# Softmax sums of two groups in one run: batched denominators in the attention of an eight-image bottleneck kernel

## The chip, the cores and the metric

The kernel runs on one core of a Trainium2 chip. The metric is device time in microseconds (us) of one execution; the figure shown for a kernel is the median of its runs. Engines are named as the profile names them: PE is TensorE (matmul), PEld its weight loads, DVE VectorE, ACT ScalarE, POOL GpSimd, and SP SyncE, whose queue issues most transfers. A matrix product in float32 goes through PE in two passes; the profile shows each pass as a record, so 8 records are 4 products.

## The reference

Eight images of 512 x 32 x 32 are normalised in groups of 16 channels, go through a convolution block with two attention bottlenecks, and are added to the input:

```python
def cbs(x, w, p, pad):
    return jax.nn.silu(bn_eval(conv2d(x, w, pad), p))

t = cbs(x, cv1_w, cv1_bn, 0)                  # 512 -> 512, split in two halves of 256 channels
ys = [t[:, :C], t[:, C:]]
for i in range(N):                            # N = 2 bottlenecks
    yi = ys[-1]
    z = cbs(yi, m_cv1_w[i], m_cv1_bn[i], 1)   # 3x3
    z = bot_attention(z, m_qkv_w[i], m_rw[i], m_rh[i])
    z = jax.nn.silu(bn_eval(conv2d(z, m_cv2_w[i], 0), m_cv2_bn[i]))
    ys.append(yi + z)
return cbs(jnp.concatenate(ys, axis=1), cv2_w, cv2_bn, 0)

# bot_attention: 4 heads of 64 channels over 1024 positions
logits = jnp.einsum('bhdi,bhdj->bhij', q, k + r) * HD ** (-0.5)
a = jax.nn.softmax(logits, axis=-1)
out = jnp.einsum('bhij,bhdj->bhdi', a, v)
# the whole: x + conv_block(group_norm(x)), group_norm over 16 channels x 1024 positions
```

The softmax's denominators are sums over the 1024 keys, one for each head and query position. The kernel takes exponentials without a maximum, multiplies by v first, and divides the result afterwards.

## The kernel before

**Rounds and attentions.** The images go in four rounds, p = 0 to 3, each with a pair: image A (`ia`) and image B (`ib`). In a round there are four attentions, in this order: A with n = 0 (first bottleneck), B with n = 0, A with n = 1, B with n = 1; 16 in all. Around each one lie the 3x3 convolution (as a Winograd product), the projection to q, k and v (as a Strassen product) and, after it, the second 1x1 product `m2` (L1270). While an attention runs, steps of other work are laid between its parts: in A and B with n = 0 the group norm of the next round's images, and in B, n = 0, the pieces that turn image A's result into Winograd tiles. The first attention of round 0 takes a path of its own to its end (`at_once`).

**One attention** (`attention_fast`, L1014) has four groups, 0 to 3: channel block c = 0 or 1 (two heads each) and half of the query positions. A group has eight key blocks, worked in four pairs. For each pair: `logits` (L1037) puts q k products in a PSUM tile of the pool with tag "big" (three tiles), ACT takes the exponentials into two `pt` tiles (L1041), `add_up` (L1055, L1057) adds them on DVE into `acc` (two buffers), and, one pair later in PE's order, `times_v` (L1071) multiplies by v into the one `av` tile of another PSUM pool. PE's order is thus logits of pair i + 1, then v of pair i.

**Border of two groups.** After a group's last v product its result is evicted: ACT copies one half of `av` (L1078), DVE adds the other (L1079); the next group's first v product needs the tile. The first `add_up` of the next group is placed behind that eviction. Ahead of the next group's first v product, PE runs `sums(g)` (L1083 to L1096): four products of a block of ones with `acc`, each on 32 columns of the array, sum it over the partitions into `s_ps`, also in the pool "big".

**From the sums to the division.** ACT copies `s_ps` to `s_row` (L1094), SP writes four rows of it to a DRAM tile (L1095). Two pairs later `spread` reads them back as 128 x 8 (`total`, L1124), DVE inverts them (L1131), SP writes them to `r_dram` (L1133) and reads each back twice (L1135), broadcast over the 64 channels of a head. `scale` (L1143) multiplies the evicted result; it is placed in the second pair of the group but one after. The last group's `sums`, `spread` and `scale` are called by the code behind the attention (`end.sums()` and so on), which puts them among the work that follows, ahead of `m2`.

**Order of work.** Instructions of an engine run in the order in which they stand in its queue. `tc.issue_after(x)` puts what follows behind instruction x in the scheduler's order. `behind` is a table of hooks: the key g, or (g, pair), names the v product behind which a step of other work is placed. `NORM_A` and `NORM_B` are the keys at which one step of the group norm (`step_norm`) is placed: four of statistics (two of `bn_stats` and one of `bn_aggr` on DVE), then the mean (`gn_mean`: a small product into a tile of the pool "big", `gm`, four DVE instructions), then `gn_rstd` (a product, `gr` L744 on DVE, a power on POOL L745, the shift on POOL L802, L803), and then the applies on ACT (L809), of which A has four of 1024 elements and B eight of 512. `at_keys` are the keys of the tile pieces (`step_part`) in B, n = 0.

Of the kernel before, what the change touches and what calls it, by code (L numbers as in the profile page):

```python
# [44 lines left out]
F32 = mybir.dt.float32  # L45
# [16 lines left out]
def kernel(  # L62
# [428 lines left out]
    def stages(act, small, ps_big, ps_av, n_pt):  # L491
# [522 lines left out]
        def attention_fast(qkv, ao, at, behind, at_once=False):  # L1014
# [66 lines left out]
            def sums(g):  # L1081

                NQ4 = HALF // 2  # L1083
                ps = ps_big.tile([P, NQ4], F32, tag="big", name="s_ps")
                acc = accs.pop(g)
                for at_q in range(4):
                    hd, part = divmod(at_q, 2)
                    nc.tensor.matmul(  # L1088
                        ps[at_q * 32 : (at_q + 1) * 32, :], ones[:, 0:32], acc[:, hd, ts(part, NQ4)],
                        start=True, stop=True, tile_position=(0, at_q * 32),  # L1090
                    )
                s_dram = tc.dram_tile([4, NQ4], F32, name=f"s_dram{at + g}")
                row = act.tile([P, NQ4], F32, tag="h", name="s_row", bufs=2)
                nc.scalar.copy(row, ps)  # L1094
                nc.sync.dma_start(s_dram, row[0:P:32, :])  # L1095
                return s_dram  # L1096
# [25 lines left out]
            def total(g, s_dram):  # L1122

                nc.sync.dma_start(sums_all[:, at + g, :], s_dram.rearrange("a (i r) -> (a i) r", r=QP))  # L1124
                return sums_all[:, at + g, :]

            def spread(g, s_dram):

                rs = act.tile([P, HALF], F32, tag="rs", name="rs", bufs=4)
                rc = small.tile([P, QP], F32, tag="rc", name="rc", bufs=2)  # L1130
                inverted[0] = nc.vector.reciprocal(rc, total(g, s_dram))  # L1131
                r_dram = tc.dram_tile([2, HALF], F32, name=f"r_dram{at + g}")
                nc.sync.dma_start(r_dram.rearrange("h (i r) -> (h i) r", r=QP), rc)  # L1133
                for hd in range(2):
                    spread_out[0] = nc.sync.dma_start(  # L1135
                        rs[hd * HD : (hd + 1) * HD, :], r_dram[hd : hd + 1, :].to_broadcast([HD, HALF])
                    )
                return rs
# [5 lines left out]

            NQ = NJ // PAIR
# [674 lines left out]
    for p in range(NP):  # L1820
# [255 lines left out]
        def step_part():  # L2076
            next(parts_at, None)
# [286 lines left out]
```

## Time and profile before

| | us |
|---|---|
| median of three runs (lowest, highest) | 2253.76 (2253.61, 2255.59) |
| the profiled execution | 2252.28 |
| its span in the trace | 2250.8 |
| PE busy | 2209.8 |
| PE: logits L1037, v products L1071 | 486.4, 485.9 |
| PE: sums L1088 (504 records) | 40.3 |
| DVE busy | 1728.8 |
| ACT busy | 1101.3 |
| POOL busy | 225.1 |

The profile is one execution. "L1088 PE MATMUL s_ps<-acc,ones ... x504 | 40.3, 391 | 2.2 <-DVE gm" reads: 504 records of line 1088 on PE that write `s_ps` from `acc` and `ones`, 40.3 us busy, 391 ns each in the mean (records overlap, since matmuls are pipelined), 2.2 us of idle time of the engine ahead of them, most of which ended with `gm` on DVE. A timeline row has start, duration, engine, line and operation; x8 in it means eight records in a row. In brackets behind a row stands the idle time ahead of it and what ended it. PE's clock was granted at 0.998 of full speed over the span.

### The profile page before, as it was taken

Reading aid. Unit: us, or ns where it says so; the run is one execution under the profiler, and the core shown is the slowest. Engines: PE = TensorE matmul, PEld = TensorE weight load, DVE = VectorE, ACT = ScalarE, POOL = GpSimd, SP = SyncE. Lnnn points to the kernel's source line nnn. Section 1 sums busy time; section 2 is a strip of 40 time slices with the busy share of each in tenths; the row PEclk is TensorE's granted clock in tenths of the full one; section 3 lists DMA queues with packets and bytes.
Section 4 is the critical chain, followed back from the end, with each engine's and each line's share of the span. In section 5 each row is a group of like instructions: output and inputs, shape, how many; then the busy total and the mean of one; then the engine's idle time right before and its main releaser. Section 6 shows DMA issues by size and latency. Waiting matters only on the chain.

```text
span 2250.8 us, 40563 instructions
## 1 busy us (share of the span) xinstructions
PE 2209.8 (98%) x16346; PEld 1079.1 (48%) x16346; DVE 1728.8 (77%) x2675; ACT 1101.3 (49%) x1359; POOL 225.1 (10%) x417
## 2 busy tenths in 40 slices
PE   7999999999999999999999999999999999999998
PEld 3653437343474445633447343654345733473443
DVE  7988879878678688877947868986794868796652
ACT  7554653644225765465324667355622455335533
POOL 4322210000220000000021000000012000000001
PEclk9999999999999999999999999999999999999999
DMA  9855447221581324521257151632136611351214
GB/s 276 309 157 150 155 148 260 91 93 50 135 269 59 113 88 143 178 64 65 66 154 260 30 173 35 198 111 82 51 79 176 226 44 34 102 192 35 67 46 111
DMA packets 135284, 285.63 MB, mean 127 GB/s; under 512 B 34512, under 2 KB 62156, under 8 KB 134064
## 3 DMA queue, kind: packets, MB, share of 16 engines
q1 hardware_dynamic: 103184, 197.34, 26.5%
q0 software_dynamic: 31904, 85.61, 13.2%
q8 instruction: 131, 2.15, 0.4%
q14 instruction: 65, 0.53, 0.1%
HBM read 214.86 MB, written 68.03 MB: 126 GB/s over the span
## 4 chain that ended last, share of the span: by engine, by line
PE 82%; DVE 11%; issue 3%; ACT 2%; DMA 1%; POOL 0%; SPq 0%; DVEq 0%; POOLq 0%; ACTq 0%
PE av_ps L1071 17%; PE l_ps L1037 16%; PE c L1290 9%; PE c_ps L653 7%; PE c_new L1290 6%; PE p_ps L916 6%; PE ps L523 5%; PE m_ps L1270 5%; PE x_ps L1390 4%; PE p_ps L922 3%; DVE acc L1057 1%; PE s_ps L1088 1%; PE p_ps L886 1%; DVE c_e L680 1%; ACT ypad L495 0%
## 5 line engine op out<-in xcount | busy, mean ns | idle before, releaser
L1041 ACT ACTIVATE pt<-l_ps 128x1024 f32<-128x1024 f32 x512 | 495.7, 1023 | 339.5 <-PE l_ps L1037 228.0
L1057 DVE TENSOR_TENSOR acc<-acc,pt 128x1024 f32<-128x1024 f32 x384 | 469.7, 1223 | 60.4 <-ACT pt L1041 34.9
L1037 PE MATMUL l_ps<-q,kr 64*64 64x512 f32 x4096 | 486.4, 590 | 2.4 <-ACT pt L1041 1.5
L1071 PE MATMUL av_ps<-pt,vT 64*64 64x512 f32 x4096 | 485.9, 591 | 1.8 <-DVE z L1079 1.5
L1037 PEld LDWEIGHTS l_ps<-q,kr 64*64 64x64 f32 x4096 | 158.0, 133 | 272.1 <-issue 251.0
L1071 PEld LDWEIGHTS av_ps<-pt,vT 64*64 64x64 f32 x4096 | 155.1, 133 | 275.3 <-issue 250.6
L653 PE MATMUL c_ps<-v_in,u 128*64 128x128 f32 x4320 | 239.1, 273 | 2.5 <-issue 2.5
L653 PEld LDWEIGHTS c_ps<-v_in,u 128*64 128x64 f32 x4320 | 235.8, 137 | 9.3 <-issue 9.3
L1270 PE MATMUL m_ps<-z,m_sb 128*128 128x512 f32 x256 | 112.5, 592 | 0.0
L658 ACT COPY c_m<-c_ps 128x512 f32<-128x512 f32 x48 | 28.1, 586 | 169.9 <-PE c_ps L653 153.1
L916 PE MATMUL p_ps<-t_z,sq 128*128 128x512 f32 x224 | 107.0, 595 | 0.0
L1079 DVE TENSOR_TENSOR z<-av_ps,z 128x512 f32<-128x512 f32 x64 | 44.0, 688 | 73.5 <-ACT z L1078 73.4
L495 ACT ACTIVATE t<-m_ps,bh,sh 128x512 f32<-128x512 f32 x64 | 46.3, 774 | 86.5 <-PE m_ps L1270 86.5
L916 PE MATMUL p_ps<-z,sq 128*128 128x512 f32 x168 | 80.1, 604 | 4.4 <-ACT z L495 4.3
L1055 DVE TENSOR_TENSOR acc<-pt 128x1024 f32<-128x1024 f32 x64 | 77.8, 1216 | 6.8 <-ACT pt L1041 6.8
L1340 POOL DMA_DIRECT2D c_out<-in_x_dram x56 | 50.3, 972 | 280.2 <-ACT c_out L495 276.8
L1270 PEld LDWEIGHTS m_ps<-z,m_sb 128*128 128x128 f32 x256 | 48.3, 190 | 58.8 <-issue 57.4
L1143 DVE TENSOR_TENSOR z<-z,rs 128x512 f32<-128x512 f32 x64 | 43.9, 686 | 26.0 <-DMA rs<-r_dram 25.9
L495 ACT ACTIVATE c_out<-cz,bh,sh 128x512 f32<-128x512 f32 x14 | 16.7, 1294 | 90.4 <-DVE cz L1367 90.4
L495 ACT ACTIVATE z<-z,bh,sh 128x512 f32<-128x512 f32 x64 | 47.7, 804 | 25.0 <-DVE z L704 24.3
L1390 PE MATMUL x_ps<-t_x,sw 128*128 128x512 f32 x128 | 55.9, 592 | 0.0
L922 PEld LDWEIGHTS p_ps<-sq,z 128*128 128x128 f32 x336 | 42.9, 191 | 26.3 <-issue 12.5
(313 smaller groups left out, 3153.7 us busy)
## 6 DMA issues: line engine op xcount, KB each, us to landing
u<-u SPq DMA_DIRECT2D x135, 512.0 KB
rs<-r_dram SPq DMA_DIRECT2D x126, 128.0 KB
sq<-sq SPq DMA_DIRECT2D x42, 384.0 KB
x<-in_x_dram SPq DMA_DIRECT2D x28, 512.0 KB
r_in<-r SPq DMA_DIRECT2D x28, 512.0 KB
y_in<-y SPq DMA_DIRECT2D x28, 512.0 KB
c_out<-in_x_dram POOLq DMA_DIRECT2D x56, 256.0 KB, 5.4
out_dram<-c_out POOLq DMA_DIRECT2D x56, 256.0 KB, 3.7
```

The costliest lines, as they stand in the source:

```text
L495: silued[0] = nc.scalar.activation(dst, src, AF.Silu, scale=sh[:, k : k + 1], bias=bh[:, k : k + 1])
L523: last_product[0] = nc.tensor.matmul(ps[:, half, :], w_of(k), rhs_of(k, half), start=(k == begin), stop=(k == end))
L653: conv_product[0] = nc.tensor.matmul(to[o], us[cp][:, k, row, c, o], rhs, start=(k == 0), stop=(k == NM - 1),)
L916: nc.tensor.matmul(ps[:, o, :], w[:, o, :], rhs, start=not onto, stop=True, skip_group_check=onto)
L922: nc.tensor.matmul(v[:, ts(j, P)], rhs[:, ts(j, P)], w[:, 2, :], start=j == 0 and not onto, stop=True, skip_group_check=True,)
L1037: nc.tensor.matmul(ps[kh * HD : (kh + 1) * HD, hd, :], kr[r, c, o : o + HD], q[r, c, ts(half, HALF)], start=True, stop=True,)
L1041: last_exp[0] = exp = nc.scalar.activation(pt, ps, AF.Exp, scale=SCALE)
L1057: ins = nc.vector.tensor_tensor(accs[g], accs[g], pt[i], ALU.add)
L1071: nc.tensor.matmul(avs[g][hd * HD : (hd + 1) * HD, kh, :], vT[r, j, o : o + HD], pt[i][r, hd, :], start=(j == 0), stop=(j == NJ - 1),)
L1270: nc.tensor.matmul(pss[half][:, oc, :], m2_sb[:, n, k, ts(oc, P)], ao[:, k, ts(half, HALF)], start=(k == 0), stop=(k == NM - 1),)
L1290: nc.tensor.matmul(ps[:, o, :], w[:, k, ts(o, P)], rhs[part][:, c], start=(k == 0 and not onto), stop=(k == KB - 1), skip_group_check=onto,)
L1390: nc.tensor.matmul(ps[:, o, :], w[:, c, ts(o, P)], rhs[c], start=(c == 0 and not onto), stop=(c == 1), skip_group_check=onto,)
```

## The change

`sums`, `total`, `spread` and `scale_all` now take a list of groups. A table `batch` says after which group which list is summed: groups 0 and 1 together, and groups 2 and 3 together; with `at_once`, and with the new argument `apart`, which B's attention with n = 0 sets, groups 2 and 3 are summed one by one, as before. A list of two groups has one `s_ps` tile of 128 x 2 x 256 and eight products in it, one copy, one transfer each of `s_dram`, `sums_all` and `r_dram`, one reciprocal of 128 x 16, and, as before, two broadcast transfers and one scale for each group. A group's sums that are batched stand where those of the list's last group stood.

A hook ("border", g) is called between the eviction of group g - 1 and the first `add_up` of group g; B's attention with n = 0 places tile pieces there, and two keys of `at_keys` are dropped. In `NORM_A` and `NORM_B` the first step moves from (0, 2) to (0, 1); in `NORM_A` (1, 3) is dropped and (3, 1) is new.

```diff
@@ -1011,7 +1011,7 @@
 
             return q, kr, vT, later
 
-        def attention_fast(qkv, ao, at, behind, at_once=False):
+        def attention_fast(qkv, ao, at, behind, at_once=False, apart=False):
 
             q, kr, vT, later = qkv
             behind.get(-1, lambda: None)()
@@ -1078,21 +1078,22 @@
                     nc.scalar.copy(dst, av[:, 0])
                     evicted[0] = nc.vector.tensor_tensor(dst, av[:, 1], dst, ALU.add)
 
-            def sums(g):
+            def sums(gs):
 
                 NQ4 = HALF // 2
-                ps = ps_big.tile([P, NQ4], F32, tag="big", name="s_ps")
-                acc = accs.pop(g)
-                for at_q in range(4):
-                    hd, part = divmod(at_q, 2)
-                    nc.tensor.matmul(
-                        ps[at_q * 32 : (at_q + 1) * 32, :], ones[:, 0:32], acc[:, hd, ts(part, NQ4)],
-                        start=True, stop=True, tile_position=(0, at_q * 32),
-                    )
-                s_dram = tc.dram_tile([4, NQ4], F32, name=f"s_dram{at + g}")
-                row = act.tile([P, NQ4], F32, tag="h", name="s_row", bufs=2)
+                ps = ps_big.tile([P, len(gs), NQ4], F32, tag="big", name="s_ps")
+                for n, g in enumerate(gs):
+                    acc = accs.pop(g)
+                    for at_q in range(4):
+                        hd, part = divmod(at_q, 2)
+                        nc.tensor.matmul(
+                            ps[at_q * 32 : (at_q + 1) * 32, n, :], ones[:, 0:32], acc[:, hd, ts(part, NQ4)],
+                            start=True, stop=True, tile_position=(0, at_q * 32),
+                        )
+                s_dram = tc.dram_tile([len(gs), 4, NQ4], F32, name=f"s_dram{at + gs[0]}")
+                row = act.tile([P, len(gs), NQ4], F32, tag="h", name="s_row", bufs=2)
                 nc.scalar.copy(row, ps)
-                nc.sync.dma_start(s_dram, row[0:P:32, :])
+                nc.sync.dma_start(s_dram.rearrange("g a i -> a g i"), row[0:P:32])
                 return s_dram
 
             def last_sums(g):
@@ -1119,29 +1120,38 @@
                 nc.sync.dma_start(cs, s_dram.rearrange("k h (i r) -> (h i) k r", r=QP))
                 nc.vector.tensor_tensor(sums_all[:, at + g, :], cs[:, 0], cs[:, 1], ALU.add)
 
-            def total(g, s_dram):
-
-                nc.sync.dma_start(sums_all[:, at + g, :], s_dram.rearrange("a (i r) -> (a i) r", r=QP))
-                return sums_all[:, at + g, :]
-
-            def spread(g, s_dram):
-
-                rs = act.tile([P, HALF], F32, tag="rs", name="rs", bufs=4)
-                rc = small.tile([P, QP], F32, tag="rc", name="rc", bufs=2)
-                inverted[0] = nc.vector.reciprocal(rc, total(g, s_dram))
-                r_dram = tc.dram_tile([2, HALF], F32, name=f"r_dram{at + g}")
-                nc.sync.dma_start(r_dram.rearrange("h (i r) -> (h i) r", r=QP), rc)
-                for hd in range(2):
-                    spread_out[0] = nc.sync.dma_start(
-                        rs[hd * HD : (hd + 1) * HD, :], r_dram[hd : hd + 1, :].to_broadcast([HD, HALF])
-                    )
-                return rs
+            def total(gs, s_dram):
+                dst = sums_all[:, at + gs[0] : at + gs[0] + len(gs), :]
+                nc.sync.dma_start(dst, s_dram.rearrange("g a (i r) -> (a i) g r", r=QP))
+                return dst
+
+            def spread(gs, s_dram):
+
+                rc = small.tile([P, len(gs), QP], F32, tag="rc", name="rc", bufs=2)
+                inverted[0] = nc.vector.reciprocal(rc, total(gs, s_dram))
+                r_dram = tc.dram_tile([len(gs), 2, HALF], F32, name=f"r_dram{at + gs[0]}")
+                nc.sync.dma_start(r_dram.rearrange("g h (i r) -> (h i) g r", r=QP), rc)
+                rss = []
+                for n in range(len(gs)):
+                    rs = act.tile([P, HALF], F32, tag="rs", name="rs", bufs=4)
+                    for hd in range(2):
+                        spread_out[0] = nc.sync.dma_start(
+                            rs[hd * HD : (hd + 1) * HD, :], r_dram[n, hd : hd + 1, :].to_broadcast([HD, HALF])
+                        )
+                    rss.append(rs)
+                return rss
 
             def scale(g, rs):
                 c, half = groups[g]
                 dst = ao[:, c, ts(half, HALF)]
                 return nc.vector.tensor_tensor(dst, dst, rs, ALU.mult)
 
+            def scale_all(gs):
+                for g, rs in zip(gs, rss.pop(gs)):
+                    ins = scale(g, rs)
+                return ins
+
+            batch = {1: (0, 1), 2: (2,), 3: (3,)} if at_once or apart else {1: (0, 1), 3: (2, 3)}
             NQ = NJ // PAIR
             s_drams, rss, evicted = {}, {}, [None]
             for i in range(len(pairs) + 1):
@@ -1149,19 +1159,22 @@
                     added = logits(pairs[i])
                     g, at_q = divmod(i, NQ)
                     with tc.issue_after(added.ins):
-                        if at_q == NQ - 2 and g > 0:
-                            rss[g - 1] = spread(g - 1, s_drams[g - 1])
+                        if at_q == NQ - 2 and g - 1 in batch:
+                            gs = batch[g - 1]
+                            rss[gs] = spread(gs, s_drams[gs])
                         if i == 1:
                             later()
-                        if at_q == 1 and g > 1:
-                            scale(g - 2, rss.pop(g - 2))
+                        if at_q == 1 and g - 2 in batch:
+                            scale_all(batch[g - 2])
                 if i > 0:
                     g, j0 = pairs[i - 1][0]
-                    if j0 == 0 and g > 0:
-                        s_drams[g - 1] = sums(g - 1)
+                    if j0 == 0 and g - 1 in batch:
+                        s_drams[batch[g - 1]] = sums(batch[g - 1])
                     times_v(pairs[i - 1])
                     if i < len(pairs) and accs.get(pairs[i][0][0], 0) is None:
                         with tc.issue_after(evicted[0].ins):
+                            before = behind.get(("border", pairs[i][0][0]), lambda: None)() or evicted[0]
+                        with tc.issue_after(before.ins):
                             added = add_up(pairs[i])
                     with tc.issue_after(added.ins):
                         behind.get(g if j0 == 0 else (g, j0 // PAIR), lambda: None)()
@@ -1170,19 +1183,21 @@
 
             g = len(groups) - 1
             if not at_once:
-                with tc.issue_after(evicted[0].ins):
-                    scale(g - 1, rss.pop(g - 1))
+                gs = batch[g]
+                if apart:
+                    with tc.issue_after(evicted[0].ins):
+                        scale_all(batch[g - 1])
                 return SimpleNamespace(
                     evicted=evicted[0], added=added,
-                    sums=lambda: s_drams.update({g: sums(g)}),
-                    spread=lambda: rss.update({g: spread(g, s_drams[g])}),
-                    scale=lambda: scale(g, rss.pop(g)),
+                    sums=lambda: s_drams.update({gs: sums(gs)}),
+                    spread=lambda: rss.update({gs: spread(gs, s_drams[gs])}),
+                    scale=lambda: scale_all(gs),
                 )
             ps, rows, s_dram = last_sums(g)
             with tc.issue_after(added.ins):
                 behind.get(len(groups) + 1, lambda: None)()
             with tc.issue_after(evicted[0].ins):
-                scale(g - 1, rss.pop(g - 1))
+                scale_all(batch[g - 1])
             rs = act.tile([P, HALF], F32, tag="rs", name="rs", bufs=4)
             nc.vector.tensor_tensor(rs, ps[:, 1, :], rows[0], ALU.add)
             nc.vector.reciprocal(rs, rs)
@@ -1946,8 +1961,8 @@
                         calls[key].append(extra[key])
             return {key: (lambda fs: lambda: [f() for f in fs])(fs) for key, fs in calls.items()}
 
-        NORM_A = ((0, 2), (0, 3), (1, 1), (1, 2), (1, 3), 2, (2, 1), (2, 2), (2, 3), 3)
-        NORM_B = ((0, 2), (0, 3), (1, 1), (1, 2), 2, (2, 1), (2, 2), (2, 3), 3, (3, 1), (3, 2), (3, 3))
+        NORM_A = ((0, 1), (0, 3), (1, 1), (1, 2), 2, (2, 1), (2, 2), (2, 3), 3, (3, 1))
+        NORM_B = ((0, 1), (0, 3), (1, 1), (1, 2), 2, (2, 1), (2, 2), (2, 3), 3, (3, 1), (3, 2), (3, 3))
         extra = {}
         if p == 0:
             more_u = filters([(0, 1, late_taps[1]), (1, 0, load_late(1, 0, inside(Y2[0])))])
@@ -2074,10 +2089,13 @@
             parts_at = (part for i in (1, 2) for part in tiles_later(i))
 
         def step_part():
-            next(parts_at, None)
-
-        at_keys = ((1, 3), (2, 1), (2, 3), 3, (3, 2)) if more else [(g, at) if at else g for g in range(NG) for at in range(1, 4)]
+            return next(parts_at, None)
+
+        at_keys = ((2, 1), (2, 3), 3, (3, 2)) if more else [(g, at) for g in range(NG) for at in range(1, 4) if (g, at) not in ((0, 2), (1, 3))]
         behind = hooks(NORM_B, {0: 1, 1: 1, 4: 1}, {key: step_part for key in at_keys})
+        behind["border", 2] = step_part
+        if not more:
+            behind["border", 1] = step_part
         if not more:
             tops = load_tops(ib, Y1[1])
             top_w = [take(("w2", j)) for j in range(2)]
@@ -2090,7 +2108,7 @@
                     return ys[0][half][part][:, c]
                 return ys[1][half][part - 2][:, c]
 
-        end = s.attention_fast(qkv, z[:, :, 1], at_of(ib, 0), behind)
+        end = s.attention_fast(qkv, z[:, :, 1], at_of(ib, 0), behind, apart=True)
         if more:
             nxt = next_cv1(1, xs, Y1[1], ia + 3)
             nxt.begin_half()
```

## The prediction

> **What bounds the kernel now.** I read the busy shares first, then the chain of work that ended last, then the costliest groups. Page of before:
>
> ```profile
> span 2250.8 us, 40563 instructions
> PE 2209.8 (98%) x16346; PEld 1079.1 (48%) x16346; DVE 1728.8 (77%) x2675; ACT 1101.3 (49%) x1359; POOL 225.1 (10%) x417
> ...
> PE 82%; DVE 11%; issue 3%; ACT 2%; DMA 1%; POOL 0%; SPq 0%; DVEq 0%; POOLq 0%; ACTq 0%
> ```
>
> TensorE (PE) is busy for 2209.8 of 2250.8 us: 41 us are idle in all. So the change gains by taking time off PE's list, and loses where something newly arrives late at PE. Of the sums the groups say:
>
> ```profile
> L1088 PE MATMUL s_ps<-acc,ones 128*32 128x256 f32 x504 | 40.3, 391 | 2.2 <-DVE gm L734 1.4 <-DVE acc L1057 0.6
> ```
>
> 504 records are 63 sums of 8 records. What PE waits for is in its list of waits (total us, times, longest):
>
> ```profile
> PE av_ps L1071 <- DVE z L1079: 1.5, 5, 0.5
> PE l_ps L1037 <- ACT pt L1041: 1.5, 4, 0.7
> PE s_ps L1088 <- DVE gm L734: 1.4, 2, 0.7
> ```
>
> Five times the first av product of a group waits for the eviction of the group before: there is one av buffer. Border of two groups in a quiet attention, in the timeline (start, duration):
>
> ```profile
> 177.09 1.90 PE L1037 MATMUL l_ps<-q,kr 64*64 64x512 f32 x16
> 177.33 0.59 ACT L1078 COPY z<-av_ps 128x512 f32<-128x512 f32 x1
> 177.95 0.69 DVE L1079 TENSOR_TENSOR z<-av_ps,z 128x512 f32<-128x512 f32 x1
> ...
> 178.91 0.64 PE L1088 MATMUL s_ps<-acc,ones 128*32 128x256 f32 x8
> 179.48 1.95 PE L1071 MATMUL av_ps<-pt,vT 64*64 64x512 f32 x16
> ...
> 181.25 0.61 PE L1037 MATMUL l_ps<-q,kr 64*64 64x512 f32 x4
> ```
>
> From the single records, 16 records of logits or av take 1.717 us. From l (177.09) to l (181.25) is 4.16, two such runs are 3.43, so one s run costs **0.73 us**: 0.24 to its second pass and about 0.22 for that pass, and 0.11 before and 0.11 to 0.16 behind it. This s run is also cover: the eviction ends at 178.64, av starts at 179.48; without s av comes at 178.81.
>
> **The change, part by part.**
>
> *1. Merged sums.* Eleven attentions merge groups (0,1) and (2,3); image B's four n=0 attentions and round 0's first merge (0,1) alone: 11 x 2 + 5 = 27 merges. Four more products within a run that goes on anyway cost two passes of 0.22 to 0.24, thus 0.44; a run of its own costs 0.73. A merge saves 0.29: 27 x 0.29 = **-7.8 us**. SP's issues of s_dram, sums_all and r_dram fall from 63 to 36 each, and 27 reciprocals (0.20 each) leave VectorE (DVE); both lie beside PE: 0.
>
> *2. Removed cover.* Where the eviction is late already, taking s away moves no av: the 0.73 that the sum above books is not got there. From the borders one by one:
> - Round 0 B n=1, and rounds 1 and 2 B n=0, first border: eviction ends 2.52 to 2.58 after the first logits behind the last av, next av at 2.64. DVE is backed up from 797 to 818 in these; its work there is the same. Lost: 3 x 0.70 = **+2.1**.
> - Quiet borders have 0.10 of slack left (1.62 against 1.717, with the semaphore), but the weight load ahead of av carries the wait and may show: 0 to 0.1 at 21 borders, I take 0.05: **+1.0**.
> - Round 0 A n=1, third border: the eviction ends at +2.94 because a scale ahead of it in DVE's queue waits for its rs transfer until 432.07. That scale moves two groups on: **-0.7**. Round 3 B n=0: tile pieces (L578, L579) ran ahead of the eviction and now come behind it, at the new border place: **-0.3**.
>
> *3. Norm steps of A, n=0, rounds 1 and 2.* The s run waited 0.7 twice for gm L734 (it takes a PSUM slot of the same pool, third of the waits above). The mean step is now behind s and av: 2 x 0.8 = **-1.6**. But from the mean on each norm step comes about one pair later (place (1,3) is gone, (3,1) is new), and this stage already has the latest eviction of all:
>
> ```profile
> 727.89 1.04 POOL L745 TENSOR_TENSOR gr<-gr,mhalf 128x4 f32<-128x4 f32 x1 [59.75 <-DVE gr L744]
> 729.01 1.21 POOL L802 TENSOR_TENSOR shift<-gm,gr 128x4 f32<-128x4 f32 x1
> 730.32 1.27 POOL L803 TENSOR_SCALAR shift<-shift 128x4 f32<-128x4 f32 x1
> 731.63 1.24 ACT L809 ACTIVATE x<-x,shift,gr 128x1024 f32<-128x1024 f32 x1 [1.80 <-POOL shift L803]
> ...
> 737.52 1.25 ACT L809 ACTIVATE x<-x,shift,gr 128x1024 f32<-128x1024 f32 x1
> 738.65 0.60 ACT L1078 COPY z<-av_ps 128x512 f32<-128x512 f32 x1
> 739.28 0.69 DVE L1079 TENSOR_TENSOR z<-av_ps,z 128x512 f32<-128x512 f32 x1 [2.92 <-ACT z L1078]
> ...
> 740.03 0.66 PE L1071 MATMUL av_ps<-pt,vT 64*64 64x512 f32 x4 [0.48 <-DVE z L1079]
> ```
>
> ScalarE (ACT) runs in order, and the apply at 737.52 held the eviction up; av came 3.01 after the logits. In the new order two applies stand ahead of that eviction, the first waits for the shift, and exponentials lie between. Counting from the logits of pair (2,1): gv on PE +8.1, gr +9.7, POOL's three rows 3.5 us, so the first apply at +13.5 to +14.8, exponentials to 16.7, second apply to 17.9, eviction to 19.2. av then comes at +4.1 after its logits. The two shift rows decide: 1.2 us each beside DVE's adds, but 0.20 where DVE was idle in other stages. The Trainium skill (GPSIMD Engine Reference, "8. Key points") says that GpSimd shares its SBUF interfaces with VectorE and contends with instructions that read two SBUF inputs; every add L1057 is one, and adds run back to back there. By that rule and this row +1.1 per border; had the shifts the short 0.20 row, 2 us less and the eviction even 0.8 earlier than before. With an apply more or less in front up to +1.6. I take +0.8, nearer the row of this very place. Added to the s cover that is not got: 2 x (0.73 + 0.8) = **+3.1**.
>
> *4. Ends of attentions with (2,3) merged.* Scale of group 2 used to be done by the attention's end; now it waits for group 3's sum, its row copy, three transfers and the broadcast, and the product m2 (L1270) waits for it. Round 1's A n=1, today with one group:
>
> ```profile
> 1002.77 0.64 PE L1088 MATMUL s_ps<-acc,ones 128*32 128x256 f32 x8
> 1004.19 0.52 SPq L1095 DMA_DIRECT2D s_dram<-s_row  x1
> 1005.82 0.31 SPq L1124 DMA_DIRECT2D sums_all<-s_dram  x1
> 1008.09 0.20 DVE L1131 RECIPROCAL rc<-sums_all 128x8 f32<-128x8 f32 x1 [3.67 <-DMA sums_all<-s_dram]
> 1011.06 1.10 SPq L1135 DMA_DIRECT2D rs<-r_dram  x2
> 1014.77 1.45 PE L1270 MATMUL m_ps<-z,m_sb 128*128 128x512 f32 x3
> 1015.82 0.68 DVE L1143 TENSOR_TENSOR z<-z,rs 128x512 f32<-128x512 f32 x1
> ```
>
> The broadcast lands 3.7 to 4.1 after its issue (other broadcasts with a scale at once behind them), so about 1014.9, m2 + 0.1. The product that reads group 2 comes after two m2 products (0.43 each). In the new order of PE's list a p_ps product (1.05 for its eight records, as in these stages) stands between at five ends (A n=1, and round 3's A n=0), so group 2 must be scaled by m2 + 1.93; at the four ends of B n=1 a c product does, + 2.58. DVE could have it scaled at m2 + 1.8 (u_z and u_zv run to 1015.9, the scale then to 1016.5) and, at B n=1 behind t_in L1352, at m2 + 2.05 to 2.9. What grows: row copy 0.38 to 0.57 (+0.19), two SP issues more for the second group (1.1 us, behind the first's), and twice as many 32-byte pieces in two transfers. For these the Trainium skill speaks against the change: its page DMA: Bandwidth & Descriptors ("Specifications") puts the least size for full rate at 512 bytes; but its fixed 2 us a transfer ("Anatomy of one DMA") would add only 0.01 for 4 KB more. The trace: s_dram in rows of 1 KB takes 1.63 from issue to the next issue, sums_all with 128 pieces of 32 bytes 2.27 to the reciprocal. By the fixed cost the doubling is 0; by the row at most 0.64 more in each, 1.3 together. I take 0.3 each: rs at m2 + 0.1 + 0.2 + 0.6 = m2 + 0.9, before DVE is free; DVE sets the end, and group 3's scale 0.6 later is about even with its product. Stall 0 to 0.3, say 0.15 at nine ends: **+1.3** (range 0 to 5). Rounds 1 and 2 A n=0 have 14 us between s and m2: 0.
>
> *5. acc and the rest.* acc has two buffers, so group 2's first add waits for the merged s to read group 0, about 1.1 us later than today. Queued behind it on DVE are two adds and the border's tile pieces; exponentials have six pt buffers (three pairs), DVE is busy for 10.1 of a group's 14.5 us. 0; without that cover at most 1 us at the two tight B n=1 attentions.
>
> Sum: -7.8 + 2.1 + 1.0 - 0.7 - 0.3 - 1.6 + 3.1 + 1.3 = **-2.9 us**. The profiled execution took 2252.28 (span 2250.8, 1.5 around it), 1.5 below the median of the runs, 2253.76. Applied to the median: **2250.8**.
>
> **Rivals.** 0.2% (4.5 us) is about what a measurement of this kernel tells from no change.
> - *A, as summed*, "half the gain is given back at late evictions": 2249.5 to 2254. Chance 0.42.
> - *B, evictions and norm come in time.* Shifts short (norm borders 2 x (0.73 - 0.8) = -0.1), quiet borders and ends covered: -7.8 + 2.1 - 0.7 - 0.3 - 1.6 - 0.1 = -8.4, so 2245.4; half-way to A 2248. For it: 4.4 us of DVE slack per group. Against: the 737.52 row. 0.38.
> - *C, slower: the broadcast is late at the nine ends.* One mechanism: rs for group 2 behind 32-byte pieces. For it: 1.6 to 2.7 us per step of the chain already. It begins to stall with rs later than m2 + 1.2 (plus 0.69 of the scale is 1.93). Landed at m2 + 2.6 the stalls are 5 x 1.4 + 4 x 0.7 = 9.8 in place of 1.3: +5.6, 2259.4. It outweighs the gain from about m2 + 1.9 on (4.2 in place of 1.3: +0). Against: chain grows 0.8 by my rows. 0.12.
> - *D, the change does not do it*: the scheduler keeps other work between the eight sum products, or acc's wait backs DVE up in every attention (0.2 x 27 = 5.4), so saved passes reappear as waits: -2.9 + 5.4 = +2.5: 2256. 0.08.
>
> **How the numbers follow.** Faster by over 0.2% needs under 2249.25: nearly all of B and a tail of A: 0.45. Slower, over 2258.3: part of C and little of D, and what I cannot see of a moved queue: 0.15. Rest 0.40. The range reaches from B's 2245.5 to the gentle end of C, 2257.5. A's own is 2249.5 to 2254.
>
> **What would show it.** s_ps records 504 still, but in 36 runs, each merged run about 1.2 us; the wait of s_ps on gm gone; PE's wait on z L1079 longer than 1.5 us, at A n=0 of rounds 1 and 2 about 2 x 2.3; PE's wait on the scale at m_ps 0 to 0.3 at each of the nine ends; first applies of the norm 13.5 to 15 us after logits (2,1). Wrong it would be by m_ps waits above 1 us each (C), evictions on time in the norm stage (B), or merged s runs longer than 1.3 us.

## The result, and the profile after

The changed kernel takes 2251.36 us (median of 22 runs, 2249.52 to 2253.13); the kernel before, on the same chip, 2254.23 (22 runs, 2253.35 to 2256.13). The ratio is 0.9986, with a 95% interval of 0.9979 to 0.9992: 3.2 us faster, between 1.8 and 4.7. The forecast was 2250.8 and -2.9.

The page after, with the busy shares and the chain, and the group of the sums:

```profile
span 2246.8 us, 40264 instructions
PE 2200.9 (98%) x16346; PEld 1080.6 (48%) x16346; DVE 1728.7 (77%) x2648; ACT 1099.6 (49%) x1332; POOL 224.4 (10%) x417
...
PE 85%; DVE 11%; issue 1%; ACT 1%; DMA 1%; SPq 0%; POOL 0%; DVEq 0%; ACTq 0%; POOLq 0%
```

```profile
L1089 PE MATMUL s_ps<-acc,ones 128*32 128x256 f32 x504 | 34.7, 386 | 0.0
```

The same 504 records, now without idle time ahead of them: the waits for `gm` are gone. DVE has 27 instructions less, all of them reciprocals. What PE waits for (total, times, longest):

```profile
PE p_ps L916 <- ACT z L495: 5.2, 6, 0.9
PE av_ps L1071 <- DVE z L1079: 4.9, 5, 1.6
```

The wait for an eviction has grown from 1.5 to 4.9, with the longest at 1.6: most of what was given back shows there. A border with a merged run, in the timeline of the changed kernel:

```profile
176.43 1.90 PE L1037 MATMUL l_ps<-q,kr 64*64 64x512 f32 x16
176.68 0.58 ACT L1078 COPY z<-av_ps 128x512 f32<-128x512 f32 x1
177.80 0.68 DVE L1079 TENSOR_TENSOR z<-av_ps,z 128x512 f32<-128x512 f32 x1
178.26 1.07 PE L1089 MATMUL s_ps<-acc,ones 128*32 128x256 f32 x16
...
179.26 1.95 PE L1071 MATMUL av_ps<-pt,vT 64*64 64x512 f32 x16
```

Even an eviction that DVE starts late, as here (177.80; ACT was done at 177.26), hides under the longer run: it ends at 178.48, and v starts at 179.26. From logits to v it is 2.83 here, against 2.40 with a single run in the kernel before. At a border without a run it is 1.72:

```profile
706.76 1.90 PE L1037 MATMUL l_ps<-q,kr 64*64 64x512 f32 x16
708.47 1.90 PE L1071 MATMUL av_ps<-pt,vT 64*64 64x512 f32 x16
```

**A measure finer than the execution's time.** Two pieces that no edit touches differ over the fourteen traces: the start-up ahead of the first v product (150.6 to 152.7 us) and what lies between PE's last product (`g_ps`, the count behind the last layer) and the end (9.0 to 11.7). What is between those two marks, from the start of the first v product to the start of `g_ps`, is called the stretch from here on. The changed kernel took 2086.77 for it in its first profile and 2087.26 in a second; the kernel before took 2090.81 in its only one. So the stretch is shorter by 4.0 or 3.6, and the experiments are compared by it beside their times. The time holds a third piece, outside the traced span. It is 1.4 to 1.6 us in every execution of the kernel before whose span is on record, and 1.5 to 3.3 in those of the changed kernel (in the mean 2.2 and 2.4 in its two measurements). Why is not known; 0.7 to 0.9 us of the gain is lost there. The second profile is from a control that ran beside three of the experiments:

> The changed kernel once more, as the yardstick for the three others on the same chip: 0.9986 of the kernel before, as in its own measurement. The stretch from the first border of the first attention to the last border of the last attention (1990.8 us in the first profile) repeats within 0.5 us; what differs between executions lies ahead of it, in the start-up.

It came to 0.9984, and its stretch was 0.5 us longer than the first (the expectation named another stretch, between two borders).

The borders of the two traces give the terms of the forecast one by one (av after logits, after less before; a run taken away is worth 0.73, since an attention with two runs gone and one doubled is 1.03 shorter, and 2 x 0.73 - 0.43 = 1.03):

| term | forecast | measured |
|---|---|---|
| 27 merges | -7.8 | 27 x 0.30 = -8.1 |
| three borders with DVE backed up | +2.1 | 0.35 + 0.89 + 0.54 = +1.8 |
| quiet borders | +1.0 | 0 |
| round 0 A n=1; round 3 B n=0 | -1.0 | -0.66 - 0.27 = -0.9 |
| gm waits | -1.6 | 2 x 0.92 = -1.8 |
| third border of A n=0, rounds 1 and 2 | +3.1 | 2 x 1.24 = +2.5 |
| ends with groups 2 and 3 merged | +1.3 | +0.7, at the next attention's first logits |
| not foreseen | | +0.8 (L916 waits for ACT z once more; perhaps chance, see below), +0.5 (`gv` in round 0's B, n=0) |

They add up to -4.5 against the -4.0 of the stretch; 0.5 is left without a place.

### The profile page after: what moved, and what is told of

Read it like the earlier page. It is cut to its first block, busy times and chain, and to the rows that moved or that the text cites. A ratio compares the mean times of both kernels' runs of the same rounds, so it can differ in the third digit from the quotient of the medians.

```text
span 2246.8 us, 40264 instructions
## 1 busy us (share of the span) xinstructions
PE 2200.9 (98%) x16346; PEld 1080.6 (48%) x16346; DVE 1728.7 (77%) x2648; ACT 1099.6 (49%) x1332; POOL 224.4 (10%) x417
## 4 chain that ended last, share of the span: by engine, by line
PE 85%; DVE 11%; issue 1%; ACT 1%; DMA 1%; SPq 0%; POOL 0%; DVEq 0%; ACTq 0%; POOLq 0%
PE av_ps L1071 18%; PE l_ps L1037 18%; PE c L1305 9%; PE c_ps L653 7%; PE c_new L1305 6%; PE p_ps L916 6%; PE ps L523 5%; PE m_ps L1285 5%; PE x_ps L1405 4%; PE p_ps L922 3%; PE s_ps L1089 1%; DVE acc L1057 1%; DVE c_e L680 1%; PE p_ps L886 1%; DVE c_t L673 1%
## 5 line engine op out<-in xcount | busy, mean ns | idle before, releaser
L916 PE MATMUL p_ps<-t_z,sq 128*128 128x512 f32 x224 | 107.0, 595 | 0.0
L1055 DVE TENSOR_TENSOR acc<-pt 128x1024 f32<-128x1024 f32 x64 | 78.0, 1219 | 18.0 <-PE s_ps L1089 11.2
L495 ACT ACTIVATE t<-m_ps,bh,sh 128x512 f32<-128x512 f32 x64 | 46.3, 773 | 91.2 <-PE m_ps L1285 91.2
L916 PE MATMUL p_ps<-z,sq 128*128 128x512 f32 x168 | 80.1, 604 | 5.3 <-ACT z L495 5.2
L495 ACT ACTIVATE c_out<-cz,bh,sh 128x512 f32<-128x512 f32 x14 | 16.8, 1301 | 89.1 <-DVE cz L1382 89.1
L495 ACT ACTIVATE z<-z,bh,sh 128x512 f32<-128x512 f32 x64 | 47.6, 804 | 25.8 <-DVE z L704 25.2
```

The costliest lines, as they stand in the source:

```text
L495: silued[0] = nc.scalar.activation(dst, src, AF.Silu, scale=sh[:, k : k + 1], bias=bh[:, k : k + 1])
L916: nc.tensor.matmul(ps[:, o, :], w[:, o, :], rhs, start=not onto, stop=True, skip_group_check=onto)
```

## The experiments

The theory to be tested: a merge is worth 0.30 us of PE, evictions and the norm's steps decide at a few borders how much of it stays, and the ends of attentions are near the point at which a later broadcast costs time. The rivals: the moved steps carry the gain; the ends are dear; or the ends are free. All times below are set beside runs of the kernel before on the same chip. Stretches are from one profile each.

| kernel | median, us | ratio (95%) | stretch, us |
|---|---|---|---|
| before | 2254.23 | | 2090.81 |
| changed, again | 2250.88 | 0.9984 (0.9975 to 0.9993) | 2087.26 |
| merging alone | 2256.80 | 1.0008 (0.9999 to 1.0017) | 2091.75 |
| places alone | 2253.68 | 0.9995 (0.9986 to 1.0004) | 2090.84 |
| only 0 and 1 merged | 2249.12 | 0.9976 (0.9966 to 0.9986) | 2087.46 |
| all merged | 2252.82 | 0.9991 (0.9982 to 1.0000) | 2090.66 |
| A's applies late | 2248.09, 2247.78 | 0.9968 (0.9956 to 0.9980), 0.9969 (0.9958 to 0.9980) | 2083.80, 2084.03 |
| A's applies and B's statistics late | 2248.86 | 0.9972 (0.9961 to 0.9983) | 2084.40 |
| A's applies late, only 0 and 1 merged | 2247.15 | 0.9968 (0.9955 to 0.9980) | 2086.36 |
| shift on DVE | 2248.22 (one run) | | 2084.10 |
| late broadcast | 2267.98 (one run) | | 2104.85 |
| sums twice | 2279.93 (one run) | | 2117.02 |

The kernel before took 2254.85 beside merging alone, places alone, only 0 and 1 merged, and all merged, 2255.08 beside the control, A's applies late, both norms late and the late broadcast, and 2254.44 beside the rest; the ratios are to these. A's applies late was measured twice.

### What a run and a product in it cost

```diff
-                for at_q in range(4):
+                for at_q in (0, 1, 2, 3) * 2:
```

> The kernel before with each group's four sum products done twice in the same run, into the same tile. Four more products in a run cost 0.43 us by the borders of the changed kernel; 63 runs, of which about 5 lie at borders that a late eviction holds up anyway: +25 us. Rival (the run's fixed part, changing the array's tiling, is the price, and products in it are nearly free): under +10; or each product costs a quarter of the 0.73 of a run: +43.

The stretch grew by 26.2 us, the single time lies 25.5 over the median before. (0.8 of the 26.2 is a wait in other work, see the next part.) At a quiet border of this kernel:

```profile
178.93 1.90 PE L1037 MATMUL l_ps<-q,kr 64*64 64x512 f32 x16
180.76 1.07 PE L1088 MATMUL s_ps<-acc,ones 128*32 128x256 f32 x16
181.76 1.95 PE L1071 MATMUL av_ps<-pt,vT 64*64 64x512 f32 x16
```

Logits to v is 2.83 against 2.40: 0.43 for four more products, at all quiet borders. So four products cost 0.43 and the run around them 0.30. At most borders that a late eviction held up anyway the four were free or cheap: -0.06 at round 0's A, n=1, -0.12 and -0.11 at the third borders of A, n=0 in rounds 1 and 2, 0.16 to 0.20 at the first ones of B, n=0 in rounds 1 to 3. That is the same cover, read from the other side. One exception is the first border of round 0's B, n=1, also late (2.64), where they cost 0.44; why is not known. The two rivals, under +10 and +43, are out.

### Merging alone, and the places alone

The first is the changed kernel with the old `NORM_A`, `NORM_B` and `at_keys` and no border hooks:

```diff
-        NORM_A = ((0, 1), (0, 3), (1, 1), (1, 2), 2, (2, 1), (2, 2), (2, 3), 3, (3, 1))
+        NORM_A = ((0, 2), (0, 3), (1, 1), (1, 2), (1, 3), 2, (2, 1), (2, 2), (2, 3), 3)
...
-        behind["border", 2] = step_part
```

> The changed kernel with the old places of the norm steps and tile pieces, so the merging alone. My theory (each merge is worth 0.30 us of PE, and the moved steps matter at five borders only): against the changed kernel the first border of round 3's B, n=0 gets its late eviction back (+0.95), the merged sum of A, n=0 in rounds 1 and 2 waits for gm again (+0.94 twice), and the eviction of the border behind it is 0.5 earlier (-0.5 twice): +1.8 us over the changed kernel, a span near 2248.6 and about 2 us under the kernel before. Rival (the moved steps carry the whole gain): no faster than the kernel before. Rival (they only cost): faster than the changed kernel.

It missed: the stretch is 4.5 to 5.0 longer than that of the changed kernel, and 0.9 longer than before. Three attentions hold all of the loss against the changed kernel: A, n=0 of rounds 1 and 2 (+1.86 and +2.07) and B, n=0 of round 3 (+1.20, forecast 0.95). The first of them, in the timeline of this kernel:

```profile
724.92 1.07 PE L1089 MATMUL s_ps<-acc,ones 128*32 128x256 f32 x16 [0.27 <-ACT pt L1041]
725.63 1.23 DVE L1055 TENSOR_TENSOR acc<-pt 128x1024 f32<-128x1024 f32 x1 [2.18 <-PE s_ps L1089]
...
728.29 1.23 DVE L1057 TENSOR_TENSOR acc<-acc,pt 128x1024 f32<-128x1024 f32 x1
729.43 0.15 DVE L736 TENSOR_TENSOR dev<-dev 128x4 f32<-128x4 f32 x1
729.62 0.16 DVE L737 TENSOR_TENSOR dev<-dev,mv 128x4 f32<-128x4 f32 x1
729.93 0.23 PE L725 MATMUL gv_ps<-dev,gmat 64*64 64x4 f32 x2 [1.23 <-DVE dev L737]
```

The merged sum releases `acc` late, DVE idles for 2.18 us ahead of the group's first add, the adds then stand between the four small steps of the norm, and PE waits 1.23 for the last of them, since its next product is `gv`. (It waits 0.53 more for the statistics ahead of the mean's product, before these rows.) This is the wait that the prediction costed at nothing. It costs nothing only where no step of other work stands behind it on DVE that PE needs soon.

The places alone are the kernel before with the new norm keys, tile keys and border hook:

> The kernel before with only the moved norm steps and tile pieces, and every group's sums on their own. My theory: the two gm waits go (-0.94 twice), the borders behind them are later by 0.5 (twice), round 3's B, n=0 gains only 0.27, as its own sum covers the rest: -1.2 us, a span near 2249.6. Third borders of A, n=0 in rounds 1 and 2: av 3.5 us after the logits, with the sum hidden under it. Rival (places carry the gain): -3 to -4 us.

The three attentions concerned became 0.97 shorter (-0.35, -0.34, -0.28), near the 1.2 expected. The stretch as a whole is unchanged (+0.03): 0.95 more was spent in the work ahead of round 1's A, n=0. There `p_ps` L916 waits 0.87 for ACT's z, and in the trace of the kernel before it does not. But this wait is also in the trace of sums twice, which moves no step (first the kernel before, then sums twice; total, times, longest):

```profile
PE p_ps L916 <- ACT z L495: 4.3, 5, 0.9
PE p_ps L916 <- ACT z L495: 5.5, 7, 0.9
```

Every trace but that of the kernel before has it, at 0.75 to 0.87; in round 3 the two traces of the changed kernel have 0 and 0.53 of it. So it can be chance that the one trace of the kernel before lacks it. Then that stretch is about 0.8 short, and merging alone stands at about 0, the places alone at -0.8 and the changed kernel at -4.3 to -4.9 against it. No second trace of the kernel before is there to decide it.

The measured ratio of the places alone, 0.9995, has 1 in its interval, as has that of merging alone. So neither part makes the gain: +0.9 and 0.0 alone, -3.6 to -4.0 together, as the stretches stand. What the places are worth depends on the merging: 4.5 to 5.0 with it, about 1 without.

### How much of it comes from groups 2 and 3

```diff
-            batch = {1: (0, 1), 2: (2,), 3: (3,)} if at_once or apart else {1: (0, 1), 3: (2, 3)}
+            batch = {1: (0, 1), 2: (2,), 3: (3,)}
```

> Groups 0 and 1 merged in all attentions, groups 2 and 3 in none. My theory: nine merges lost at 0.30 each (+2.7), the two at the late third borders of A, n=0 cost nothing to lose and give 0.43 back each at the end (-0.9), and the later first logits behind the ends of A, n=1 go (-0.6): +1.2 us over the changed kernel. Rival (ends are free, every merge counts): +3.3. Rival C (ends are dear): faster than the changed kernel by over 1 us.

The times seem to say the opposite of the theory, 0.9976 against 0.9986 and 0.9984, but the intervals overlap. The stretch is 0.2 to 0.7 longer than the changed kernel's, below the 1.2 expected. Inside, the terms are as forecast: +0.73 at each third border that gets its own run back, 0 at the two that are late; at the ends -0.43, and -0.66 in all behind A, n=1. (One more border moved: the first of round 0's B, n=1 came at 2.58 instead of 2.26.) A merge of groups 2 and 3 is thus worth 0.30 at B, n=1, 0.07 at A, n=1, and it costs 0.43 at A, n=0 of rounds 1 and 2, as long as that border is late.

The same pair again, beside each other and with that border mended (next part):

> A's applies late, and only groups 0 and 1 merged. My theory (a merge of groups 2 and 3 is worth 0.30 now also at A, n=0 of rounds 1 and 2, whose third border isn't late any more; at A, n=1 it is worth about 0, as the next attention's first logits take 0.22 to 0.23 back): the stretch is 1.5 to 2 us longer than with A's applies late alone, and the time not less. Rival (the first measurement with only groups 0 and 1 merged was right by the clock, merging 2 and 3 costs): 2 us less than with the applies late alone.

The stretch is 2.3 to 2.6 longer without the merges of groups 2 and 3; the times are the same, 2247.15 and 2247.78. From PE's last product to the end it took 9.0 in the one and 11.7 in the other. Those 2.7 us lie behind all that was changed; all four profiles in which A's applies were late with all merges in place, or merging was alone, have 11.2 to 11.7 there, the others 9.0 to 9.6. In these four PE's last drain, at the program's last line, comes 2.2 to 2.7 us behind the instruction of PE ahead of it, in the others 0.1 to 0.6; what holds it up was not found. So on PE the merges of groups 2 and 3 are worth something more than the 1.5 to 2 expected, and in the measured time it isn't shown that they are worth anything.

The other direction, all groups merged in B, n=0 too:

```diff
-        end = s.attention_fast(qkv, z[:, :, 1], at_of(ib, 0), behind, apart=True)
+        end = s.attention_fast(qkv, z[:, :, 1], at_of(ib, 0), behind)
```

> Groups 2 and 3 merged in B, n=0 too. My theory: four more merges are -1.2 us on PE, but a scale of 0.69 more stands in DVE's queue at each of these ends, where DVE is backed up and PE waits for what follows: +0.7 each, and up to 1 us more each if the second broadcast is late; +1.6 us over the changed kernel, 0 to +5. Rival (the end has room): -1.2.

Stretch +3.4 to +3.9 over the changed kernel, within the 0 to +5 and above the +1.6. The four third borders became 0.68 shorter; behind the ends of rounds 1 and 2 it was 3.0 longer each. There a wait of x_ps for ACT (0.6) and one of c_ps (1.7) are new, the latter ending 0.7 us after the last tile pieces (DVE L608). The scales on DVE are not what delayed these pieces. In round 1 PE's list has changed: the changed kernel runs m2's 16 records in a row from 869.71, while here 4 of them are followed by 4 of x_ps and the other 12 come from 874.07. The activation behind m2 (ACT L495) starts at 876.84 instead of 873.35, DVE waits 1.33 for it, and the tile pieces end 2.6 later. So the theory had the right sign and the wrong path.

### The late eviction of A, n=0

```diff
-        NORM_A = ((0, 1), (0, 3), (1, 1), (1, 2), 2, (2, 1), (2, 2), (2, 3), 3, (3, 1))
+        NORM_A = ((0, 1), (0, 3), (1, 1), (1, 2), 2, (2, 1), 3, (3, 1), (3, 2), (3, 3))
```

> The changed kernel with the four applies of A's norm placed one to two pairs later, all behind the third border's eviction. My theory (the eviction of A, n=0 in rounds 1 and 2 is late because an apply stands ahead of it on ACT, and that costs 1.8 us each): av comes 1.72 instead of 3.52 us after the logits, twice, -3.6 us. Rival (the applies are needed by what follows the attention): the same there, but the x_ps products behind the end start later by 1 to 3 us each, and the time is the same or more.

First the border in the changed kernel, then with the applies late:

```profile
735.56 1.96 PE L1037 MATMUL l_ps<-q,kr 64*64 64x512 f32 x16
736.60 1.23 ACT L809 ACTIVATE x<-x,shift,gr 128x1024 f32<-128x1024 f32 x1
737.73 0.58 ACT L1078 COPY z<-av_ps 128x512 f32<-128x512 f32 x1
738.34 0.69 DVE L1079 TENSOR_TENSOR z<-av_ps,z 128x512 f32<-128x512 f32 x1 [4.82 <-ACT z L1078]
739.08 1.95 PE L1071 MATMUL av_ps<-pt,vT 64*64 64x512 f32 x16 [1.57 <-DVE z L1079]
```

```profile
736.08 1.96 PE L1037 MATMUL l_ps<-q,kr 64*64 64x512 f32 x16
736.38 0.59 ACT L1078 COPY z<-av_ps 128x512 f32<-128x512 f32 x1 [0.64 <-PE av_ps L1071]
737.00 0.69 DVE L1079 TENSOR_TENSOR z<-av_ps,z 128x512 f32<-128x512 f32 x1 [2.97 <-ACT z L1078]
737.79 1.96 PE L1071 MATMUL av_ps<-pt,vT 64*64 64x512 f32 x16
```

3.52 became 1.72, twice: -3.6, and nothing behind the attention gave it back (x_ps starts as before). The stretch is 3.0 to 3.5 shorter than the changed kernel's, and the time 0.9968 of the kernel before, 2.8 us under the changed kernel on the same chip. A second measurement agrees:

> The changed kernel with A's four applies behind the third border's eviction, once more, beside the next: by the first measurement 0.9968 of the kernel before, and 3.0 us less than the changed kernel in the stretch of the attentions.

So the version that beats both kernels costs one line. The second reason for a late eviction was tried with it, B's fourth step of statistics behind the first border:

```diff
-        NORM_B = ((0, 1), (0, 3), (1, 1), (1, 2), 2,
+        NORM_B = ((0, 1), 1, (1, 1), (1, 2), 2,
```

> The same, and in B's norm the fourth step of statistics behind the first border instead of ahead of it. My theory (DVE's backlog makes that border's eviction late in rounds 1 and 2 of B, n=0, and 1.49 us of it are these statistics): av 1.72 to 1.9 instead of 2.80 and 2.44 after the logits, -1.6 us more, thus -5.2 against the changed kernel in the stretch of the attentions. Rival (the backlog is only moved: the mean and the root behind it come late and PE waits for gm or gv): these waits grow by 1 us each, and nothing is gained over the kernel with A's applies late.

Nothing was gained: round 1's and round 2's first border of B, n=0 stayed at 2.44 and 2.45, as with A's applies late alone, and the attentions of B, n=0 in rounds 0 to 2 are 0.16 to 0.20 longer. But the run does not test its theory. With A's applies late alone the fourth step's statistics (DVE L718) already stood behind the eviction (in round 1 at 817.85, the eviction at 816.11); the edit moved them to 820.65. The third step's, ahead of the eviction at 812.25, stayed where they were. Whether statistics make this eviction late therefore stays open, and so does what else DVE's backlog of 797 to 818 us in the kernel before is made of.

The forecast had said that POOL's two shift rows decide:

```diff
-            nc.gpsimd.tensor_tensor(shift, gm, gr, ALU.mult)
-            shifted[0] = nc.gpsimd.tensor_scalar(shift, shift, -1.0, None, ALU.mult)
+            shifted[0] = stt(shift, gm, -1.0, gr, ALU.mult, ALU.mult)
```

> The changed kernel with the norm's shift made by one instruction on DVE in place of two on POOL. My theory of the prediction (the two POOL rows, slowed beside DVE's adds, decide when the first apply starts and so how late the third eviction of A, n=0 is): the first apply comes 1.5 to 2 us earlier, and av at that border 0.8 to 1.2 us earlier than 3.52. Rival (the eviction is late because an apply stands ahead of it, whenever the shift is made): av moves by less than 0.3.

```profile
731.03 1.04 POOL L745 TENSOR_TENSOR gr<-gr,mhalf 128x4 f32<-128x4 f32 x1 [64.26 <-DVE gr L744]
732.11 0.16 DVE L802 SCALAR_TENSOR_TENSOR shift<-gm,gr 128x4 f32<-128x4 f32 x1 [1.17 <-POOL gr L745]
732.45 1.24 ACT L808 ACTIVATE x<-x,shift,gr 128x1024 f32<-128x1024 f32 x1
...
735.89 1.24 ACT L808 ACTIVATE x<-x,shift,gr 128x1024 f32<-128x1024 f32 x1
```

The lines are one lower from here on, as the edit takes a line away. Counted from the logits of pair (2,1), which start at 721.21 here and at 720.49 in the changed kernel, the first apply starts at 11.2 instead of 13.2 us, and av at that border at 2.11 instead of 3.52: -1.41 each, more than forecast. Both causes are real: the order on ACT costs 1.80 (3.52 against 1.72), and 1.41 of it goes away when the shift is in time, though the applies stay where they are.

### How near the ends are

```diff
+                if gs[0] == 2 and len(gs) == 2:
+                    hop = tc.dram_tile([len(gs), 2, HALF], F32, name=f"hop{at}")
+                    nc.sync.dma_start(hop, r_dram)
+                    r_dram = hop
```

> The changed kernel with one more copy between two DRAM tiles in the chain of groups 2 and 3, ahead of the broadcast; the result is the same. It adds the time of one small transfer, about 2 us by the rows of this chain (1.6 to 2.7). My theory (the scale of group 2 lies on m2's path with little room: at A, n=1 and round 3's A, n=0 DVE sets it and rs has about 1 us, at B, n=1 rs sets it already): m2 stalls of 1.0 at five ends and 1.5 at four, +11 us, at least +6. Rival (the end has room, the broadcast is not critical): under +3.

The stretch grew by 18 us, above the +11; it is not where it was expected. Behind the first three ends of B, n=1 nothing grew, behind the last +0.7. Behind A, n=1 it is +2.2, +4.3, +4.1 and +2.1 up to the end of the next attention, behind round 3's A, n=0 +2.0, and behind the two ends with 14 us of room +1.1 and +0.9. Round 1's A, n=1 first in the changed kernel, then with the copy:

```profile
1007.04 0.25 DVE L1131 RECIPROCAL rc<-sums_all 128x16 f32<-128x16 f32 x1 [4.44 <-DMA sums_all<-s_dram]
1010.41 3.01 SPq L1138 DMA_DIRECT2D rs<-r_dram  x4
1014.27 1.88 PE L1285 MATMUL m_ps<-z,m_sb 128*128 128x512 f32 x4
1015.32 0.68 DVE L1147 TENSOR_TENSOR z<-z,rs 128x512 f32<-128x512 f32 x1
1015.99 0.38 PE L922 MATMUL p_ps<-sq,t_z 128*128 128x128 f32 x2
1016.21 2.31 PE L1285 MATMUL m_ps<-z,m_sb 128*128 128x512 f32 x5
```

```profile
1015.58 0.53 SPq L1136 DMA_DIRECT2D hop<-r_dram  x1
1017.55 2.38 SPq L1142 DMA_DIRECT2D rs<-hop  x4
1019.15 1.88 PE L1289 MATMUL m_ps<-z,m_sb 128*128 128x512 f32 x4
...
1020.87 1.05 PE L922 MATMUL p_ps<-sq,t_z 128*128 128x128 f32 x8
1022.57 1.28 DVE L1151 TENSOR_TENSOR z<-z,rs 128x512 f32<-128x512 f32 x2
1023.67 0.59 PE L1289 MATMUL m_ps<-z,m_sb 128*128 128x512 f32 x1
```

PE does not stall at m2 here: the scheduler has laid more of the projection's products between m2's blocks, and with them PE bridges the time. The price shows behind it, at the next attention's first logits, which now wait for q on DVE (1.3) and for the exponentials of the first pairs (1.3). PE does wait for the scale at m2 in three other places: 0.80 and 0.60 behind the two ends with 14 us of room, and 0.49 behind the last B, n=1. So the ends are near, as the theory had it, but at the dearest of them what is late next is not m2.

## Why the prediction was right

The forecast's sum was -2.9 and the measured ratio says -3.2 (the stretch -3.6 to -4.0). Mechanism, sign and most terms held; that the two numbers lie 0.3 apart is in part luck. The terms that were foreseen measure -5.8 together: none is off by more than 1.0, but all but one of the misses lie on the same side. What brings the time back to -3.2 was not foreseen: 1.3 us of waits in the traces (of which 0.8 may be chance), 0.5 without a place, and 0.7 outside the traced span.

**Merged sums (step 1)** held to 0.3 us: 0.73 a run, 0.43 for four more products, and the experiment with sums done twice confirms the second in the measured time. **Removed cover (step 2)** held border by border, with one term mis-sized: the weight load ahead of av, taken as 0.05 at 21 borders, showed nothing; av comes at 1.72 at every quiet border.

**The norm (step 3)** was right in its place and its sign. The eviction behind two applies came at 3.52, where the sum took 3.8 and the hand count 4.1: the first apply started 13.2 us after the logits, below the stated 13.5 to 14.8, because one shift row took 0.81. The gm waits were worth 0.92 each, not 0.8. What the Trainium skill says of GpSimd and VectorE sharing their SBUF interfaces (GPSIMD Engine Reference, "8. Key points"), which the forecast had weighed, agrees with these rows: in round 1 the two shift rows took 0.81 and 1.27 beside DVE's adds in the changed kernel, and 0.20 and 0.23 where DVE was idle (merging alone).

**The ends (step 4)** came to about half the stall, 0.7 in place of 1.3, by another path. Three of its numbers failed. The chain hardly grew with the 32-byte pieces: in round 1's A, n=1 it took 5.32 from the sum to the reciprocal before and 5.21 after. Wherever the reciprocal waits for the transfer of the sums, it starts 1.52 to 1.71 us after the issue with 128 pieces (ten of twelve cases before; the row that the forecast used, 2.27, is one of the other two, and the last took 3.96), and 1.66 to 1.84 with 256 (eight cases after, 1.63 to 2.07 in its second trace). So a fixed cost describes it, with 0.1 to 0.2 for the doubling in place of 0.3. (The Trainium skill, DMA: Bandwidth & Descriptors, "Anatomy of one DMA", states its fixed 2 us for transfers issued from GpSimd; these are issued from SyncE.) The four broadcast issues took 2.4 to 3.0 us instead of the 2.2 implied. And the need at m2 + 1.93 was right only as a sum: a product of m2 takes 0.86 (four records in 1.72), not 0.43, and the p_ps product between takes 0.22, not 1.05. What the term came to, +0.7, lay at the following attention's first logits, behind A, n=1 of rounds 0 to 2 (0.22 to 0.23 each), and not at m2.

**acc and the rest (step 5)** was right for the kernel as changed and wrong as a reason. "Six pt buffers and DVE slack" does not cover the wait in general: with the old places of the norm the two attentions concerned are 2 us longer each. The cover was the place of the norm steps, which the forecast had booked under another heading.

Of the rivals, B (everything in time) did not happen, but the one-line variant comes near it: 2248.09 and 2247.78 us against the 2245.4 to 2248 named. C, the late broadcast, did not happen, but it was a real danger: two us more in the chain cost 18. D's second half, the wait for `acc` backing up DVE, is what merging alone does, in two attentions.

## What to carry to other kernels

When a short piece of work is taken from the engine that bounds, look border by border at what it was hiding; a merge is worth the fixed part of a run (0.30 of 0.73 here), and the cover it leaves behind is worth the whole run where a wait comes out. Two edits that are worth little or nothing alone (+0.9 and 0.0) can be worth 4 us together, so a part shouldn't be thrown out on its own measurement. And where a gain of a thousandth is timed, take the stretch between two marks on the bounding engine out of the trace too: in the two kernels that were traced twice it repeated within 0.5 and 0.2 us, while start-up and wind-down differ by 2 and 2.7 over all traces. Trace the kernel before twice as well: here one wait of 0.8 us in its single trace is left undecided.

## What was not expected of the hardware

Reading 256 pieces of 32 bytes back took hardly longer than 128 (medians of 1.71 and 1.84 us in two traces against 1.62, from issue to reciprocal, where it waits for them). One power of 128 x 4 on POOL takes 1.03 to 1.13 us wherever it stands, while each of the two multiplications behind it takes 0.19 to 0.24 with DVE idle, and 0.81 to 1.28 where it starts beside one of DVE's adds; then it ends about when the add does. From PE's last product to the end of the program it took 9.0 to 9.6 us in ten profiles and 11.2 to 11.7 in four, of kernels whose code there is the same; the two kernels that were traced twice kept to one side each. Why stays open.
